# A large-kernel convolution behind an attention block: the normalization's shift put into the tap strips with a product on GpSimd and one addition on VectorE, and a last store in three transfers

## The chip, the cores and the metric

The kernel runs on one core of a Trainium2 chip. The metric is the device time of one execution in microseconds; the time before is the median of three runs.

In the names of the profile PE is TensorE (matmuls), PEld its weight loads, DVE VectorE, ACT ScalarE, POOL GpSimd, SP SyncE (here a queue that issues transfers). A name with a q behind it (SPq, POOLq) is an engine's sequencer, which issues transfers and waits for semaphores.

## What is computed

The input is one image of 384 channels and 192 x 192 pixels. The first layer adds an attention block over the channels to its normalized input (not touched here). The second normalizes its input in 32 groups, sends it through seven depthwise convolutions, each with its own batch normalization, and adds their sum to the input:

```python
x = x + _L0_conv_ref(_gn(x), ...)
x = x + _L1_conv_ref(_gn(x), ...)

def _L1_conv_ref(x, w0, ..., bn6):          # BRANCHES: (5,1) (7,1) (5,2) (3,3) (3,4) (3,5)
    out = bn_apply(dwconv(x, w0, 1), bn0)   # w0: 13 x 13
    for (k, r), w, bn in zip(BRANCHES, ws, bns):
        out = out + bn_apply(dwconv(x, w, r), bn)
    return out
```

Everything is float32. The seven convolutions fit into 13 x 13 taps, so the kernel merges them, with the batch normalizations, into one set of taps for each channel.

## The kernel before

The first 1960 us hold the statistics and the attention block; from there to 2108 us the projection (line 1459) runs, and the convolution of the second layer from 2108 us to the end. It is worked off in `NK` = 48 chunks of `CC` = 8 channels. In a chunk, a partition stands for one of `UQ` = 4 row phases, a channel and one of `NE` = 4 row ranges.

For a chunk k, these steps follow each other, spread over several iterations of the loop:

- `load_rows(k)` (lines 1288 and 1295): eight transfers on SP's queue bring the rows of the input (`raw`) and of the projection (`up`). `raw` has three buffers, `up` two. For the last chunk, one row is first cleared by a memset on POOL (line 1274).
- `load_taps(k)` (line 1310): one transfer on SP's queue brings the chunk's strips `wt` of 256 columns for each channel, three buffers. For chunk 1 it is two transfers of half the channels.
- `residual(k)` (line 1328): `raw` plus `up`, on POOL; each value of `up` is read twice in a row with a zero step. For chunks 0 and 1 it runs on DVE in pieces of 3 rows (576 elements) and a last one of 1 (192).
- `normalize1(k, i)` (line 1336), i = 0, 1, 2: scale and bias on ACT, the long part and two edge rows, into `xn` (two buffers).
- `arrange(k)` (line 1351): two DVE stream transposes from `xn` into the patches `xp` (two buffers).
- `patch(k)` (line 1318): the identity of the residual has to go through the convolution too. For this, the strips get, in the middle row block (`PAD * BC` on, 64 columns), the fixed pattern `mask` times a number for each channel, `sdb[:, cc]`, which depends on the normalization. It is eight DVE instructions of 64 columns, `w = mask * sdb + w`. The numbers `sdb` and the biases `cb` are made by `derive`, for each third of the channels, while the loops run.
- `convolve(k, c, co)` (line 1371): for each of the 8 strips c (a strip is a channel's taps), 8 matmuls; the result goes from PSUM (`l_ps`, four buffers) by an ACT eviction (line 1379) with the bias `cb` into `co` (two buffers).
- `finish(k, co, lo)` (lines 1412 and 1421): one DVE stream transpose of `co` into `o` (two buffers), and four stores on POOL's queue, one for each row phase, 32 partitions of 288 KB.

The order on every engine is the order in the program (`manual_schedule`). Iteration k of the loop on line 1530 issues `load_rows(k + 3)`, `load_taps(k + 2)` and `residual(k + 2)`, and then for c = 0 to 7 `convolve(k, c)`. At c = 0 stand, on DVE, `arrange(k + 1)`, `patch(k + 1)` and the transpose of `finish(k - 1)`, whose stores follow on POOL. The three parts of `normalize1(k + 2)` stand behind the evictions of c = 3, 4, 5 (in iteration 0: 5, 6, 7). In iteration 0, `patch(1)` is done in two halves, at c = 6 and 7. `patch(0)` lies in the projection's loop, at step `NBB + 20`.

The last chunk is convolved in two halves of the rows (`convolve_part`, line 1390, evictions on line 1403). The first half, three row blocks, is transposed and stored beside the second half's matmuls; the second half's three row blocks are transposed as two and one behind the last eviction, each with four stores over the queues of SP, ACT, POOL and SP.

Of the kernel before, what the change touches and what calls it, by code (L numbers as in the profile page):

```python
# [7 lines left out]
F32 = mybir.dt.float32  # L8
AF = mybir.ActivationFunctionType
ALU = mybir.AluOpType  # L10
# [4 lines left out]
P = 128  # L15
# [3 lines left out]
HW = H * W  # L19
# [9 lines left out]
PAD = K0 // 2  # L29
# [4 lines left out]
UQ = 4  # L34
MR = H // UQ
BR, BC = 8, 16
NT, NBQ = H // BR, W // BC
NQ = MR + 3
CC = 8
NE = 4  # L40
ME = MR // NE
TE = NT // NE
WP = W + 16
ZS = (K0 + UQ - 1) * BC
MH = UQ * BC
# [13 lines left out]
def tile_attn_then_large_kernel_conv(ctx: ExitStack, tc: tile.TileContext, a: dict, out: bass.AP):  # L59
    nc = tc.nc  # L60
    x = a["x"]
# [170 lines left out]
    o = 3 * ZQ * K0 * BC + (UQ - 1) * BC  # L232
# [58 lines left out]
    with (  # L291
# [6 lines left out]
            out=bn.rearrange("p j q i -> p j (q i)"), in_=a["bn"].rearrange("(j p) s -> p j s", p=P)  # L298
# [13 lines left out]
        for i, (k, _) in enumerate(((K0, 1),) + BRANCHES):  # L312
            wb = s1.tile([P, NJ, k, k], F32, name=f"wb{i}")
            nc.gpsimd.dma_start(
                out=wb.rearrange("p j a b -> p j (a b)"), in_=a[f"w{i}"].rearrange("(j p) s -> p j s", p=P)
# [7 lines left out]
        def load_blocks():  # L323
# [31 lines left out]
            out=wd[:, :nqk], in_=a["w_dw"][: nqk * P].rearrange("(m p) t -> p m t", p=P)  # L355
# [148 lines left out]
        for n in range(NJ * NX):  # L504
# [43 lines left out]
            if j < 2 and b == NX - 16:  # L548
                w = P * (j + 1)
# [43 lines left out]
    with ctx_v:  # L593
# [716 lines left out]
                eng.dma_start(out=wt[:, c : c + n], in_=zds[j][c0 : c0 + n].rearrange("c p z -> p c z"))  # L1310
                yield

        def patch(k, lo=0, hi=CC):

            for c in range(lo, hi):
                cc = k * CC + c
                w = taps[k][:, c, PAD * BC : (PAD + UQ) * BC]
                nc.vector.scalar_tensor_tensor(
                    w, mask.rearrange("p u x -> p (u x)"), sdb[:, cc : cc + 1], w, ALU.mult, ALU.add
                )  # L1320

        def residual(k, eng=nc.gpsimd, n=ME + 1):

# [81 lines left out]
        def finish(k, co, lo, parts=((0, TE),), engines=(nc.gpsimd,), o=None):  # L1405


            if o is None:
                o = lo.tile([P, TE, 2, W], F32, tag="o", name=f"o_{k}")
            for t0, n in parts:  # L1410
                at, of = o[:, t0], co[:, :, t0, :]
                nc.vector.transpose(  # L1412
                    bass.AP(at.tensor, at.offset, [list(at.ap[0]), [2 * W, n], [BC, NBQ], [W, 2], [1, BC]]),
                    bass.AP(
                        of.tensor,
                        of.offset,
                        [list(of.ap[0]), [NBQ, n], [1, NBQ], [NT * NBQ, CC], [TE * NBQ, NE]],
                    ),
                )
                for u in range(UQ):  # L1420
                    engines[u % len(engines)].dma_start(  # L1421
                        out=bass.AP(
                            out.tensor,
                            out.offset + k * CC * HW + (2 * u + t0 * BR) * W,
                            [[ME * UQ * W, CC * NE], [BR * W, n], [1, 2 * W]],
                        ),
                        in_=o[u * 32 : (u + 1) * 32, t0 : t0 + n].rearrange("p t y w -> p t (y w)"),
                    )
            return o
# [14 lines left out]
        with (  # L1444
            tc.tile_pool(name="by", bufs=3) as by,
            tc.tile_pool(name="b2_ps", bufs=3, space=PSUM) as b2_ps,
        ):
            stats1 = l1.tile([P, NJ, NBB, 6], F32, name="stats_t")

            for n in range(NJ * NBB):  # L1450
                i, b = divmod(n, NBB)
                if n + 4 < NJ * NBB:
                    load_sum(n + 4)
                if b == 0 and i > 0:
                    running.append(derive(i - 1, stats1))
                advance()
                ps = b2_ps.tile([P, NBK], F32, tag="pj", name="pj")
                for j in range(NJ):
                    nc.tensor.matmul(  # L1459
                        ps,  # L1460
                        lhsT=wp[:, j, i * P : (i + 1) * P],
                        rhs=v[:, j, b * RB : (b + 1) * RB, :].rearrange("p r w -> p (r w)"),
                        start=(j == 0),
                        stop=(j == NJ - 1),
                    )
                pj = by.tile([P, 2, RB // 2, WS], F32, tag="pjs", name="pjs", bufs=6)
                nc.scalar.activation(
                    pj.rearrange("p y r w -> p r y w"),
                    ps.rearrange("p (r y w) -> p r y w", y=2, w=WS),
                    AF.Identity,  # L1470
                    bias=bpj[:, i : i + 1],
                )
                t = by.tile([P, NBK], F32, tag="cell", name="cell", bufs=1)
                sm = smj.pop(n)
                nc.vector.scalar_tensor_tensor(t, sm, quarter[:, i : i + 1], ps, ALU.mult, ALU.add)
                nc.vector.bn_stats(stats1[:, i, b, :], t)
                if i == 0:
                    nc.vector.bn_stats(stats_s[:, i, b, :], sm)
                pd = pds[i]
                nc.scalar.dma_start(  # L1480
                    out=bass.AP(
                        pd.tensor,
                        pd.offset + b * NBK // 2,
                        [[HS // 2 * WS, P], [P * HS // 2 * WS, 2], [1, NBK // 2]],
                    ),
                    in_=pj.rearrange("p y r w -> p y (r w)"),
                )
                if n == NBB + 8:
                    running.append(load_rows(0, nc.gpsimd))
                if n == NBB:  # L1490
                    running.append(load_taps(0, nc.gpsimd, 1))
                if n == NBB + 14:
                    running.append(residual(0, nc.vector, 3))
                if n == NBB + 20:
                    assert not running
                    patch(0)
                    for q in range(3):
                        normalize1(0, q)
                    first = arrange(0, 1)
                if n > NBB + 20 and n % 3 < 2:  # L1500
                    next(first, None)

                if n == NBB + 22:
                    running.append(load_rows(1, nc.gpsimd))
                if n == 2 * NBB + 8:
                    second = residual(1, nc.vector, 3)
                if n >= 2 * NBB + 8 and (n % 3 == 2 or n > 2 * NBB + 16):
                    next(second, None)
                if n == 3 * NBB - 4:
                    assert next(first, first) is first and next(second, second) is second  # L1510
                if n >= 3 * NBB - 4 and n < 3 * NBB - 1:
                    normalize1(1, n - (3 * NBB - 4))
            while running:
                advance()
            running.append(derive(NJ - 1, stats1))
            advance()
# [3 lines left out]
    with (  # L1520
        tc.tile_pool(name="l2", bufs=1) as l2,
        tc.tile_pool(name="more", bufs=1) as more,
        tc.tile_pool(name="lo", bufs=2) as lo,
    ):
        pools["more"] = more
        patches(l2, 1)
        all_of(load_rows(2))
        all_of(load_taps(1, n=CC // 2))
        last = None
        for k in range(NK):  # L1530
            if k + 3 < NK:
                all_of(load_rows(k + 3))
            if k + 2 < NK:
                all_of(load_taps(k + 2))
                all_of(residual(k + 2))
            co = lo.tile([P, CC, NT, NBQ], F32, tag="co", name=f"co_{k}")
            for c in range(CC):
                if k < NK - 1:
                    convolve(k, c, co)
                else:  # L1540
                    convolve_part(k, c, co, 0, TE // 2)
                if c == CC - 2:
                    advance()
                if c == 0:
                    if k + 1 < NK:
                        all_of(arrange(k + 1))
                        if k > 0:
                            patch(k + 1)
                    if last is not None:
                        finish(k - 1, last, lo)  # L1550

                if k == 0 and c >= CC - 2:
                    patch(1, (c - CC + 2) * CC // 2, (c - CC + 3) * CC // 2)
                n = c - (CC - 3 if k == 0 else 3)
                if 0 <= n < 3 and k + 2 < NK:
                    normalize1(k + 2, n)
            last = co
        engines = (nc.sync, nc.scalar, nc.gpsimd, nc.sync)
        o = None
        for c in range(CC):  # L1560
            convolve_part(NK - 1, c, last, TE // 2, TE // 2)
            if c == 0:
                o = finish(NK - 1, last, lo, ((0, TE // 2),))
        finish(NK - 1, last, lo, ((TE // 2, 2), (TE // 2 + 2, 1)), engines, o)
        ctx_p.close()
    ctx_l1.close()

# [48 lines left out]
```

## Time and profile before

| | us |
|---|---|
| time, median of 3 runs | 2867.17 (2865.95 to 2869.23) |
| the profiled execution: time | 2862.88 |
| its span, first to last instruction | 2861.1 |
| of it from the first convolution matmul (2108.23) on | 752.9 |

Busy time of the engines in three stretches of the span (us from its start), with the mean share of the 16 DMA engines (transfers that overlap on one engine count twice):

| stretch | PE | DVE | ACT | POOL | DMA share | GB/s |
|---|---|---|---|---|---|---|
| 2030 to 2100 | 68.47 | 61.29 | 22.36 | 4.63 | 0.77 | 219 |
| 2500 to 2600 | 100.00 | 97.58 | 43.06 | 50.25 | 1.07 | 271 |
| 2800 to 2861 | 53.33 | 45.67 | 21.48 | 17.05 | 0.58 | 155 |

The groups of instructions that the change touches or stands beside, by line and form:

| line, engine, instruction | form | count | busy us | mean ns |
|---|---|---|---|---|
| L1318 DVE SCALAR_TENSOR_TENSOR, `wt` | 128x64 | 384 | 79.6 | 286 |
| L1351 DVE STREAM_TRANSPOSE, `xp` | 128x4608, whole chunk | 47 | 394.5 | 8394 |
| L1412 DVE STREAM_TRANSPOSE, `o` | 128x2304 | 47 | 206.4 | 4391 |
| L1328 POOL TENSOR_TENSOR, `raw` | 128x2496 | 46 | 230.0 | 5001 |
| L1328 DVE TENSOR_TENSOR, `raw` | 128x576 | 8 | 5.9 | 743 |
| L1328 DVE TENSOR_TENSOR, `raw` | 128x192 | 2 | 0.7 | 346 |
| L280 POOL TENSOR_TENSOR, `sum` | 128x192 | 128 | 87.9 | 687 |
| L281 POOL TENSOR_TENSOR, `sum` | 128x192 | 128 | 100.9 | 789 |
| L1421 POOL issue of a store, `out` | | 194 | 107.4 | 582 |

How to read it: the lines that follow in the next part are rows of the same profile. A row of a timeline has the start and the length in us, the engine, the line of the kernel, the instruction, what it writes from what it reads, the shape, how often (merged), and in brackets how long the engine was idle before and what ended that. A row of the waits has who waited for whom, the total in us, how often, and the longest.

### The profile page before, as it was taken

To read this page: it belongs to the slowest core of one execution; us is meant where nothing else is said; L and a number is where in the kernel's file an instruction comes from. 1 tells how busy PE (TensorE), PEld (TensorE's weight loads), DVE (VectorE), ACT (ScalarE), POOL (GpSimd) and SP (SyncE) were. 2 spreads that over 40 slices of the span, in tenths; PEclk is the share of its full clock that TensorE was granted. 3 is DMA by queue.
4 is the path that set the end of the run, shared out by engine and by line. 5 is a ranking of instruction groups with operands and counts; after the bars stand their busy time and mean duration, and the time that the engine had idled before them with its cause. 6 is when DMAs were issued, how large, how long until landed. Compare 5 with 4: busy or idle time off the path is not lost.

```text
span 2861.1 us, 37738 instructions
## 1 busy us (share of the span) xinstructions
PE 2735.6 (96%) x13662; PEld 1677.2 (59%) x13662; DVE 2498.5 (87%) x3484; ACT 1332.9 (47%) x2427; POOL 917.3 (32%) x1129
## 2 busy tenths in 40 slices
PE   0699999999999999999999999999999999999998
PEld 0356666666666666666655555545566666666666
DVE  6879998888878888788899998888789999999997
ACT  3755554444444444454444444444334444444443
POOL 4251231332323223241222222232114445444443
PEclk9899999999999999999999999999999999999999
DMA  9942432232422324232333333328889999999996
GB/s 389 419 151 65 134 114 87 81 126 72 135 74 92 111 70 137 67 126 81 100 108 107 108 109 116 115 69 234 234 206 282 270 275 275 256 271 271 270 275 168
DMA packets 269561, 475.75 MB, mean 166 GB/s; under 512 B 25858, under 2 KB 189968, under 8 KB 269248
## 3 DMA queue, kind: packets, MB, share of 16 engines
q1 hardware_dynamic: 204208, 301.51, 38.2%
q0 software_dynamic: 43328, 149.04, 15.5%
q10 hardware_dynamic: 21840, 22.81, 2.3%
q8 instruction: 108, 1.77, 0.3%
q14 instruction: 77, 0.63, 0.1%
HBM read 337.06 MB, written 136.20 MB: 165 GB/s over the span
## 4 chain that ended last, share of the span: by engine, by line
PE 85%; DVE 7%; DMA 5%; ACT 1%; issue 1%; POOL 0%; ACTq 0%; SPq 0%; DVEq 0%; POOLq 0%
PE qkv L671 51%; PE conv L1371 24%; PE pj L1459 4%; DVE v L719 3%; DMA xs<-in_x 3%; PE gram L760 2%; PE tr L748 2%; PE av L1131 1%; DVE mx L683 1%; PE qkv L429 1%; DVE acc L719 1%; DVE stats L535 1%; DMA v<-in_x 0%; DMA smj<-sums 0%; DMA wt<-zd 0%
## 5 line engine op out<-in xcount | busy, mean ns | idle before, releaser
L671 PE MATMUL qkv<-xt,wqk 128*128 128x384 f32 x3304 | 1082.5, 486 | 1.9 <-DVE mx L683 1.1
L671 PEld LDWEIGHTS qkv<-xt,wqk 128*128 128x128 f32 x3304 | 620.1, 190 | 417.1 <-DVE mx L683 4.5
L719 DVE SCALAR_TENSOR_TENSOR acc<-pooled,wd,acc 128x384 f32<-128x384 f32 (+2 forms) x1152 | 733.7, 637 | 30.6
L1371 PE MATMUL conv<-xp,wt 128*64 128x288 f32 (+1 forms) x6016 | 723.9, 404 | 2.4 <-issue 1.7
L690 ACT ACTIVATE pooled<-mx,bq 128x192 f32<-128x192 f32 x432 | 196.8, 456 | 900.2 <-DVE mx L683 898.1
L1371 PEld LDWEIGHTS conv<-xp,wt 128*64 128x64 f32 x6016 | 462.9, 137 | 260.8 <-issue 2.7
L683 DVE TENSOR_REDUCE mx<-qkv 128x192 f32<-128x768 f32 x432 | 412.3, 954 | 200.1 <-PE qkv L671 187.1
L671 PE MATMUL qkv<-xt,wv 128*128 128x384 f32 x1728 | 562.4, 487 | 2.5 <-DVE mx L683 2.2
L671 PEld LDWEIGHTS qkv<-xt,wv 128*128 128x128 f32 x1728 | 326.0, 190 | 233.4 <-DVE mx L683 9.8
L1351 DVE STREAM_TRANSPOSE xp<-xn 128x4608 f32<-128x4608 f32 (+1 forms) x107 | 445.4, 4163 | 18.0 <-PE conv L1371 10.6
L280 POOL TENSOR_TENSOR sum<-xt 128x192 f32<-128x192 f32 x128 | 87.9, 687 | 969.0 <-ACT xt L651 968.0
L719 DVE SCALAR_TENSOR_TENSOR v<-pooled,wd,v 128x384 f32<-128x384 f32 (+2 forms) x576 | 375.4, 652 | 15.2
L1379 ACT ACTIVATE co<-conv,cb 128x288 f32<-128x288 f32 x376 | 186.9, 497 | 386.1 <-PE conv L1371 381.3
L651 ACT ACTIVATE xt<-xt,gn 128x768 f32<-128x768 f32 x278 | 275.5, 1014 | 0.0
L1328 POOL TENSOR_TENSOR raw<-raw,up 128x2496 f32<-128x2496 f32 x46 | 230.0, 5001 | 38.2 <-DMA up<-pd 27.6
L1421 POOL DMA_DIRECT2D out<-o x194 | 107.4, 582 | 373.5 <-DVE o L1412 315.2
L1412 DVE STREAM_TRANSPOSE o<-co 128x2304 f32<-128x2304 f32 (+3 forms) x50 | 211.0, 4222 | 9.6 <-ACT co L1403 8.8
L1459 PE MATMUL pj<-v,wp 128*128 128x384 f32 x432 | 142.6, 489 | 1.0 <-ACT v L1138 0.7
L788 POOL DMA_DIRECT2D zd<-v x96 | 72.0, 756 | 216.1 <-ACT v L779 216.1
L1336 ACT ACTIVATE xn<-raw,par 128x2112 f32<-128x2112 f32 x48 | 103.1, 2148 | 25.4 <-POOL raw L1328 21.8
L1459 PEld LDWEIGHTS pj<-v,wp 128*128 128x128 f32 x432 | 80.9, 190 | 55.9 <-ACT v L1138 1.4
L281 POOL TENSOR_TENSOR sum<-sum,xt 128x192 f32<-128x192 f32 x128 | 100.9, 789 | 10.8
(296 smaller groups left out, 1914.6 us busy)
## 6 DMA issues: line engine op xcount, KB each, us to landing
xt<-in_x SPq DMA_DIRECT2D x96, 1152.0 KB, 7.4
raw<-in_x SPq DMA_DIRECT2D x182, 312.0 KB, 13.2
out<-o POOLq DMA_DIRECT2D x188, 288.0 KB, 8.4
wt<-zd SPq DMA_DIRECT2D x46, 1024.0 KB, 12.2
zd<-v POOLq DMA_DIRECT2D x96, 416.0 KB, 4.4
up<-pd SPq DMA_DIRECT2D x184, 156.0 KB, 12.6
xs<-in_x POOLq DMA_DIRECT2D x20, 768.0 KB, 10.7
smj<-sums SPq DMA_DIRECT2D x72, 192.0 KB, 3.0
```

The lines of the kernel that those rows point to most:

```text
L651: nc.scalar.activation(xt[:, j], xt[:, j], AF.Identity, bias=gn0[:, j, 1:2], scale=gn0[:, j, 0:1])
L671: nc.tensor.matmul(ps[:, r, : 2 * W], lhsT=wq[:, j, mm * P : (mm + 1) * P], rhs=xt[:, j, r * 2 * W : (r + 1) * 2 * W], start=(j == 0), sto ...
L683: nc.vector.tensor_reduce(mx, ps[:, :, : 2 * W].rearrange("p r (y w x) -> p r w y x", y=2, x=2), AX.XY, ALU.max,)
L690: nc.scalar.activation(pool_t[m][:, k : k + SR, 1 : 1 + WS], mx, AF.Identity, bias=bq[:, m : m + 1])
L719: nc.vector.scalar_tensor_tensor(acc[:, :nt], pool_t[m][:, k0 + dy : k0 + dy + nt, dx : dx + WS], wd[:, m, t : t + 1], acc[:, :nt], ALU.mu ...
L1328: eng.tensor_add(rv, rv, uv.unsqueeze(2).to_broadcast([P, (m1 - m0) * WS, 2]))
L1351: nc.vector.transpose(bass.AP(at.tensor, at.offset, [list(at.ap[0]), [NBQ, n], [1, NBQ], [NQ * NBQ, CC], [ME * NBQ, NE]],), bass.AP(row.te ...
L1371: nc.tensor.matmul(ps[h * MH : (h + 1) * MH, t0:t1], lhsT=wt[:, c, o : o + MH], rhs=d[:, c, g + 2 * t0 : g + 2 * t1 - 1 : 2, :], start=(e ...
L1379: nc.scalar.activation(co[:, c], ps, AF.Identity, bias=cb[:, cc : cc + 1])
L1412: nc.vector.transpose(bass.AP(at.tensor, at.offset, [list(at.ap[0]), [2 * W, n], [BC, NBQ], [W, 2], [1, BC]]), bass.AP(of.tensor, of.offse ...
L1421: engines[u % len(engines)].dma_start(out=bass.AP(out.tensor, out.offset + k * CC * HW + (2 * u + t0 * BR) * W, [[ME * UQ * W, CC * NE], [ ...
L1459: nc.tensor.matmul(ps, lhsT=wp[:, j, i * P : (i + 1) * P], rhs=v[:, j, b * RB : (b + 1) * RB, :].rearrange("p r w -> p (r w)"), start=(j = ...
```

## The change

The eight instructions of a patch become one product and one addition. `shade(k)` forms `mask` times the eight numbers of chunk k into a new tile `part` (128 x 8 x 64, one buffer) on POOL; `patch(k)` adds `part` to the strips in one DVE instruction. `shade(0)` stands ahead of `patch(0)`, and `shade(k + 1)` at the head of iteration k. `patch(1)` is no longer done in halves. `normalize1` moves from behind c = 3, 4, 5 to behind c = 4, 5, 6, except in iteration 0. For a single row block `finish` now issues one store of all 128 partitions in place of four of 32, and the last three row blocks are transposed and stored one by one; their queues are SP, SP and ACT, by `engines[t0 % len(engines)]` with t0 = 3, 4, 5.

```diff
-        def patch(k, lo=0, hi=CC):
-
-            for c in range(lo, hi):
-                cc = k * CC + c
-                w = taps[k][:, c, PAD * BC : (PAD + UQ) * BC]
-                nc.vector.scalar_tensor_tensor(
-                    w, mask.rearrange("p u x -> p (u x)"), sdb[:, cc : cc + 1], w, ALU.mult, ALU.add
-                )
+        parts = {}
+
+        def shade(k):
+
+            part = parts[k] = l1a.tile([P, CC, MH], F32, tag="part", name=f"part_{k}")
+            flat = mask.rearrange("p u x -> p (u x)")
+            nc.gpsimd.tensor_mul(
+                part,
+                flat.unsqueeze(1).to_broadcast([P, CC, MH]),
+                sdb[:, k * CC : (k + 1) * CC].unsqueeze(2).to_broadcast([P, CC, MH]),
+            )
+
+        def patch(k):
+
+            w = taps[k][:, :, PAD * BC : PAD * BC + MH]
+            nc.vector.tensor_add(w, w, parts.pop(k))
...
+                if n == 1:
+                    engines[t0 % len(engines)].dma_start(
+                        out=bass.AP(
+                            out.tensor,
+                            out.offset + k * CC * HW + t0 * BR * W,
+                            [[2 * W, UQ], [ME * UQ * W, CC * NE], [1, 2 * W]],
+                        ),
+                        in_=o[:, t0].rearrange("p y w -> p (y w)"),
+                    )
+                    continue
...
                 if n == NBB + 20:
                     assert not running
+                    shade(0)
                     patch(0)
...
         for k in range(NK):
+            if k + 1 < NK:
+                shade(k + 1)
             if k + 3 < NK:
                 all_of(load_rows(k + 3))
...
-                if k == 0 and c >= CC - 2:
-                    patch(1, (c - CC + 2) * CC // 2, (c - CC + 3) * CC // 2)
-                n = c - (CC - 3 if k == 0 else 3)
+                if k == 0 and c == CC - 1:
+                    patch(1)
+                n = c - (CC - 3 if k == 0 else 4)
...
-        finish(NK - 1, last, lo, ((TE // 2, 2), (TE // 2 + 2, 1)), engines, o)
+        finish(NK - 1, last, lo, [(t0, 1) for t0 in range(TE // 2, TE)], engines, o)
```

## Prediction

> **What bounds the kernel now.** The change touches the convolution, from 2108 us to the end, so I read the profile for that stretch: first which waits TensorE (PE) had there, then one chunk on each engine, then the start and the end of the stretch. All the waits of PE from 2108 us on are two:
>
> ```profile
> PE conv L1371 <- issue: 1.7, 1, 1.7
> PE conv L1371 <- ACT co L1379: 0.8, 1, 0.8
> ```
>
> PE loses 2.4 us in 745 us. From 2390.07 to 2837.48 us it runs 3728 matmuls with nothing between, 0.120 us each, so 15.36 us for a chunk's 128. One chunk in the timelines of VectorE (DVE) and GpSimd (POOL):
>
> ```profile
> 2771.65 4.37 DVE L1412 STREAM_TRANSPOSE o<-co 128x2304 f32<-128x2304 f32 x1
> 2776.31 9.36 DVE L1351 STREAM_TRANSPOSE xp<-xn 128x384 f32<-128x384 f32 x2 [0.29 <-PE conv L1371]
> 2785.50 1.59 DVE L1318 SCALAR_TENSOR_TENSOR wt<-mask,sdb,wt 128x64 f32<-128x64 f32 x8
> 2786.99 4.41 DVE L1412 STREAM_TRANSPOSE o<-co 128x2304 f32<-128x2304 f32 x1
> ...
> 2776.32 2.22 POOL L1421 DMA_DIRECT2D out<-o  x4 [7.64 <-DVE o L1412]
> 2778.94 4.96 POOL L1328 TENSOR_TENSOR raw<-raw,up 128x2496 f32<-128x2496 f32 x1 [0.40 <-ACT co L1379]
> ```
>
> To be seen: DVE works 9.36 + 1.59 + 4.41 us, less small overlaps, in a chunk of 15.36 us, and its only idle time, 0.29 us, ends when PE has finished reading the old patches. So PE sets the pace and DVE follows 0.3 us behind. The strips are ready at 2787.0, and PE needs them when chunk 44 begins, about 2791.4: 4.4 us of slack.
>
> The two waits of PE lie in the first chunks:
>
> ```profile
> 2120.35 4.92 POOL L1328 TENSOR_TENSOR raw<-raw,up 128x2496 f32<-128x2496 f32 x1 [11.48 <-DMA up<-pd]
> 2122.31 4.43 DVE L1318 SCALAR_TENSOR_TENSOR wt<-mask,sdb,wt 128x64 f32<-128x64 f32 x8 [0.50 <-DMA wt<-zd]
> 2125.47 15.58 PE L1371 MATMUL conv<-xp,wt 128*64 128x288 f32 x128 [1.66 <-issue]
> 2139.21 2.15 ACT L1336 ACTIVATE xn<-raw,par 128x2112 f32<-128x2112 f32 x1 [5.31 <-POOL raw L1328]
> 2141.80 2.38 PE L1371 MATMUL conv<-xp,wt 128*64 128x288 f32 x18 [0.76 <-ACT co L1379]
> ```
>
> The first strip of chunk 1 began at 2122.31 and lasted 3.06 us (the longest of line 1318; the median is 0.28). It ended 0.09 us after POOL's addition, which ran from 2120.35 to 2125.27, and PE began 0.1 us later. The same happens at 2138.73, where eight strips take 1.91 us beside a POOL addition that ends at 2139.18. The second wait: ScalarE (ACT) stood 5.31 us at a normalization that is queued ahead of the eviction PE needed.
>
> The end:
>
> ```profile
> 2853.79 2.30 DVE L1412 STREAM_TRANSPOSE o<-co 128x768 f32<-128x768 f32 x2 [5.53 <-ACT co L1403]
> 2855.37 1.76 SPq L1421 DMA_DIRECT2D out<-o  x4
> ```
>
> Two transposes, then eight stores on three queues; SP issues the last at 2856.72 to 2857.13, waits 2.4 us for stores to land (2859.5), and the span ends 1.6 us after that.
>
> **The change on DVE.** Removed: 48 groups of eight strips, 79.6 us by the costliest groups, about 1.6 us a chunk. Added: 48 additions of 128x512. The nearest rows are DVE additions of line 1328: 0.743 us for 576 elements, 0.346 for 192, so 1.034 ns an element, and 0.346 + 320 x 1.034 ns = 0.68 us for 512. DVE gains about 0.9 us a chunk, 43 us in all. On the path this is worth nothing in the steady chunks, as DVE waits for PE there: its idle 0.29 us becomes 1.2. Only if that cover were gone (PE faster than 14.5 us a chunk) would it show. Bounds for one addition: 0.66 us (512 at the 576 row's 1.29 ns an element) to 0.92 (at the 192 row's 1.80); both below 1.59. The first patch stands in the projection, at 2052.46; what it gives back there goes into DVE's next wait, 1.30 us for ACT until 2055.40.
>
> **The change on POOL.** Added: 48 products of 128x512, with both inputs spread by zero steps, which no row shows. The rows around it are the 2496-element addition (5.00 us, 2.00 ns an element, one input spread twofold) and the sums of line 281 (0.789 us for 192, 4.11 ns). Flat, these give 1.02 and 2.10 us. I take the line through 0.687 us at 192 (line 280) and 5.00 at 2496, which gives 0.69 + 320 x 1.87 ns = 1.29 us. POOL is 40 to 50% busy in the stretch, so the place matters, not the sum. The product for chunk k+1 stands at the head of iteration k, behind the four stores of the iteration before and ahead of the residual addition (L1328) for k+2. The stores wait for DVE's output transpose, which now ends 0.9 us sooner; so the stores end 0.9 sooner, the product takes 1.29, and the addition starts 0.4 us later than now or when its rows land, whichever is last. It ends some 8.3 us into the chunk; the patch comes at 9.5, the normalization later. The wait for the single buffer `part` is short: its patch was read half a chunk before. Behind the product on POOL are also the stores, the residual and, once, the memset ahead of the last chunk's rows, for which SP's queue waits (2793.82 now); 0.4 us there is covered by those rows' consumer at 2809.28.
>
> The row for a conflict is the 3.06 us strip: a DVE operation stood until a POOL operation ended. [...]
>
> **The normalization moved** one strip later (c = 4, 5, 6). Its long part can start 10.1 us into the chunk instead of 8.2, the edges end by about 14.4 (evictions come 1.92 us apart), and the next DVE transposes need them at 15.6: nothing on the path. Its rows' buffer comes free 1.92 us later; it is refilled more than ten microseconds after that (chunk 43's buffer was normalized by 2758, reloaded from 2772.26), so SP's queue doesn't feel it.
>
> **The start.** Products 0 and 1 run on an idle POOL, before 2052 and 2111. `patch(1)`, two halves before, is one addition now and waits for both halves of the taps. The second landed at 2125.47, when SP's next load was let go; the POOL addition is over at 2125.27. So the patch ends at 2125.5 + 0.7 = 2126.2, and PE starts chunk 1 0.8 us later than now. In exchange, the eviction of c = 4 no longer stands behind the normalization, and the second wait, 0.76 us, goes. Sum: 0. Bounds: -2.4 us (both waits gone) to +1.5 (the first grows by 0.8 to 1.5, the second stays).
>
> **The end.** Three transposes of 384 columns for 768 + 384: 3 x 0.82 less two overlaps of 0.08, 2.3 us again. The stores are three of 192 KB, on SP, SP and ACT, each sent as its transpose ends, at about 2854.7, 2855.4 and 2856.2, for the first at 2855.37. ACT's stores of 192 KB in the projection landed in 3.1 us (median), 2.8 us for SP's 192 KB loads there: the last lands near 2859.0 for 2859.5. I take -0.5 us; bounds 0 (the same 589 KB need the same 2.7 us of transfer, 2856.15 to 2858.85, from the last issue) and -1.1 (all of them move from 2855.4 on). [...]
>
> **Sum.** 0 in the steady chunks, 0 at the start, -0.5 at the end: the profiled execution, 2862.88 us (span 2861.1 and 1.8 around it), becomes 2862.4. The median of the runs is 4.3 us above that execution, and I keep that distance: 2866.7 us.
>
> **Rivals.** (1) DVE, not PE, sets the pace. For it: the sum of DVE's work is within 0.3 us of the chunk. Against: the 2.4 us of PE's waits. It would give 47 x 0.9 = 42 us: 2825. Chance 0.07, with anything else that saves over 5.7 us. (2) POOL and DVE in a ring become the pace: output transpose 4.40, a gap of 0.30, stores 2.22, the product, 0.1, residual 4.97, 0.1, patch 0.68, make 12.77 us plus the product. It decides from 2.6 us for the product on; at 1.29 the ring takes 14.1, at 2.10 14.9. Should the two spread inputs make it 3.5 us, each of 46 chunks takes 0.9 us more: 41 us, 2908. For it: no row shows such inputs; against: the row with one spread input is the cheapest per element. Chance 0.13, with lesser losses above 5.7 us. (3) The start loses 1.5 us and the end gains nothing: 2868.7; chance 0.08, indistinguishable from no change. (4) The product is not ahead at all, as its patch waits for it each chunk; it has until 9.5 us and ends at about 3, so this is rival 2 in its beginnings and costs nothing below the same point.
>
> **How the numbers follow.** 0.2% of the time, 5.7 us, is about what a measurement of this kernel can tell from no change. The forecast has 0.72. The bounds at start and end sum to -3.5 and +1.5 us, 2863.7 to 2868.7; the runs reach from 1.2 us below their median to 2.1 above, so the range is 2862.5 to 2870.8. It leaves out rivals 1 and 2, 0.20 together. Faster 0.07; same 0.72 + 0.08 = 0.80; slower 0.13.
>
> **What would show it.** Right: matmuls in the steady chunks still back to back at 15.36 us, DVE's wait for PE at about 1.2 us a chunk, the POOL product at 1.0 to 2.1 us, the residual addition ending before the patch, PE's first wait near 2.5 us and no second one, the last store landing 0.5 us sooner after the last matmul. Wrong: PE waiting for the patch or for evictions in the steady chunks, a patch of over 1 us (stopped by POOL), or a product above 2.6 us.

## The result and the profile after

| | before | after |
|---|---|---|
| time, median of 21 runs each | 2865.69 (2862.84 to 2869.23) | 2870.80 (2866.60 to 2875.91) |
| after to before | | 1.0018 [1.0012, 1.0024] |
| the profiled execution: span | 2861.1 | 2869.8 |
| its first convolution matmul | 2108.23 | 2110.91 |
| from there to the last half's first matmul | 729.25 | 731.39 |
| from there to the end of the span | 23.62 | 27.50 |

The change costs 5.1 us; the interval of the ratio makes that 3.4 to 6.9 us. The spans differ by 8.7 us: 2.68 before the convolution begins, 2.14 in its chunks, 3.88 at the end. I don't put the first of these down to the change: the first convolution matmul lies between 2107.0 and 2112.6 us over the profiled executions of before, after and the twelve kernels below, with no order by edit. So I read the stretches from that matmul on, and use whole times only with their intervals.

Waits of TensorE from the convolution on; columns: engine, tile and line waiting, releaser, sum in us, times, longest:

```profile
PE conv L1379 <- issue: 3.1, 1, 3.1
```

There were two of 1.7 and 0.8; now there is one, of 3.1. The steady chunks, in TensorE's timeline:

```profile
2394.89 447.58 PE L1379 MATMUL conv<-xp,wt 128*64 128x288 f32 x3728
2842.30 0.91 PE L1398 MATMUL conv<-xp,wt 128*64 128x144 f32 x12
```

The same 3728 matmuls took 447.41 us before (2390.07 to 2837.48) and take 447.41 now (2394.89 to 2842.30). One chunk in the timelines of VectorE and GpSimd:

```profile
2774.97 0.71 DVE L1328 TENSOR_TENSOR wt<-wt,part 128x512 f32<-128x512 f32 x1
2775.56 4.42 DVE L1420 STREAM_TRANSPOSE o<-co 128x2304 f32<-128x2304 f32 x1
2780.27 2.24 POOL L1439 DMA_DIRECT2D out<-o  x4 [7.16 <-DVE o L1420]
2781.13 9.36 DVE L1359 STREAM_TRANSPOSE xp<-xn 128x384 f32<-128x384 f32 x2 [1.16 <-PE conv L1379]
2782.43 1.15 POOL L1319 TENSOR_TENSOR part<-mask,sdb 128x512 f32<-128x512 f32 x1
2783.43 5.07 POOL L1336 TENSOR_TENSOR raw<-raw,up 128x2496 f32<-128x2496 f32 x1
```

The eight instructions of 1.59 us have become one of 0.71, and all that this frees stands in the bracket of the third VectorE operation: it idles 1.16 us until TensorE has read the old patches, where it was 0.29. The residual addition ends at 2788.50; the next patch comes some 1.8 us later, so the two don't meet.

The start of the convolution, from the same timelines:

```profile
2123.10 4.93 POOL L1336 TENSOR_TENSOR raw<-raw,up 128x2496 f32<-128x2496 f32 x1 [10.54 <-DMA up<-pd]
2128.78 0.69 DVE L1328 TENSOR_TENSOR wt<-wt,part 128x512 f32<-128x512 f32 x1 [4.25 <-DMA wt<-zd]
2129.57 30.71 PE L1379 MATMUL conv<-xp,wt 128*64 128x288 f32 x240 [3.08 <-issue]
```

The one addition of chunk 1 waits for the second half of the taps (4.25 us idle), starts when they are there, and TensorE follows 0.1 us behind it. But its next 240 matmuls take 30.71 us. The same 240 take 29.02 us in e12 below, where the clock stayed whole, so 1.69 us are lost here. The same stretch cut into windows (columns: busy time and count of TensorE, granted clock with 1.00 for full speed, DMA share, GB/s):

```profile
2128.00:2130.00 2.00, 0.42 (x4) 1.00 1.09 213
2130.00:2132.00 2.00, 2.00 (x13) 0.54 1.11 218
2132.00:2134.00 2.00, 2.00 (x14) 0.61 1.08 203
2134.00:2136.00 2.00, 2.00 (x20) 1.00 1.09 277
```

For 3.4 us from 2130.1 on the granted clock is half, and 13 or 14 matmuls go where 20 went. Before, behind a gap of 1.66 us, it stayed at 1.00.

The end, in the timelines of VectorE and the queues, and in windows (busy time and count of PE, PEld, DVE, ACT, POOL; then granted clock, DMA share, GB/s):

```profile
2858.61 2.36 DVE L1420 STREAM_TRANSPOSE o<-co 128x384 f32<-128x384 f32 x3 [5.53 <-ACT co L1411]
2859.50 1.32 SPq L1429 DMA_DIRECT2D out<-o  x2
2861.00 1.15 ACTq L1429 DMA_DIRECT2D out<-o  x1
```

```profile
2862.00:2864.00 2.00, 0.00 (x0) 0.00 (x0) 0.00 (x0) 0.00 (x0) 0.00 (x0) 0.50 0.26 89
2866.00:2868.00 2.00, 0.00 (x0) 0.00 (x0) 0.00 (x0) 0.00 (x0) 0.00 (x0) 0.50 0.24 90
```

The transposes and the issues are where they were expected, the last issue 2.4 us behind the first transpose. But the transfers then move some 90 GB/s with the DMA share standing at 0.26, a quarter of the 16 engines, until 2868. Before, the like stretch had a share of 0.65 to 0.81, at 167 to 218 GB/s, and was over in 3 us. One of its windows:

```profile
2857.00:2858.00 1.00, 0.00 (x0) 0.00 (x0) 0.00 (x0) 0.00 (x0) 0.00 (x0) 0.50 0.81 218
```

### The profile page after: what moved, and what is told of

It is laid out like the page before. It is cut to its first block, busy times and chain, and to the rows that moved or that the text cites. A ratio compares the mean times of both kernels' runs of the same rounds, so it can differ in the third digit from the quotient of the medians.

```text
span 2869.8 us, 37175 instructions
## 1 busy us (share of the span) xinstructions
PE 2739.0 (95%) x13662; PEld 1680.4 (59%) x13662; DVE 2452.9 (85%) x3149; ACT 1334.1 (46%) x2427; POOL 966.4 (34%) x1175
## 4 chain that ended last, share of the span: by engine, by line
PE 85%; DVE 8%; DMA 5%; ACT 1%; issue 1%; ACTq 0%; DVEq 0%; POOL 0%; SPq 0%
PE qkv L671 51%; PE conv L1379 25%; DVE v L719 3%; PE pj L1477 3%; DMA xs<-in_x 3%; PE gram L760 2%; PE tr L748 2%; DVE mx L683 1%; PE av L1131 1%; PE qkv L429 1%; DVE acc L719 1%; DMA smj<-sums 1%; DVE stats L535 1%; PE conv L1398 1%; DMA sm<-sums 0%
## 5 line engine op out<-in xcount | busy, mean ns | idle before, releaser
L1420 DVE STREAM_TRANSPOSE o<-co 128x2304 f32<-128x2304 f32 (+2 forms) x51 | 211.1, 4143 | 10.5 <-ACT co L1411 8.8
```

What stands on the lines that cost most here:

```text
L1420: nc.vector.transpose(bass.AP(at.tensor, at.offset, [list(at.ap[0]), [2 * W, n], [BC, NBQ], [W, 2], [1, BC]]), bass.AP(of.tensor, of.offse ...
```

## The experiments

In the expectations "theory" and "rival" are those of each run. The table puts all of them side by side: the two stretches of the profiled execution, TensorE's first wait in the chunks, the median, and the ratio to the kernel before, which ran beside them on the same chip (its medians there: 2865.81 for e1 to e4, 2866.25 for e5 to e8, 2866.40 for e9 to e12). The ratio and its 95% interval are those of the measurement, not the quotient of the medians; where the two part, as for e5 and e10, neither says much alone.

| kernel | to the last half | from there to the end | first wait | median (runs) | ratio to before |
|---|---|---|---|---|---|
| before | 729.25 | 23.62 | 1.66 | | |
| after | 731.39 | 27.50 | 3.08 | 2870.80 (21) | 1.0018 [1.0012, 1.0024] |
| e1 | 735.87 | 23.68 | 3.78 | 2866.57 (11) | 1.0001 [0.9990, 1.0011] |
| e2 | 730.26 | 27.50 | 1.60 | 2869.26 (12) | 1.0012 [0.9996, 1.0028] |
| e3 | 728.84 | 27.51 | 2.03 | 2868.00 (11) | 1.0013 [1.0001, 1.0025] |
| e4 | 731.27 | 21.83 | 2.96 | 2864.35 (11) | 0.9994 [0.9986, 1.0003] |
| e5 | 731.05 | 23.06 | 3.11 | 2866.61 (11) | 1.0010 [0.9998, 1.0021] |
| e6 | 732.72 | 23.71 | 0 | 2863.96 (11) | 0.9993 [0.9984, 1.0002] |
| e7 | 728.26 | 23.56 | 1.52 | 2866.20 (1) | |
| e8 | 742.11 | 27.28 | 2.92 | 2878.32 (4) | 1.0049 [1.0035, 1.0063] |
| e9 | 730.72 | 27.15 | 2.42 | 2869.86 (12) | 1.0010 [0.9999, 1.0020] |
| e10 | 729.96 | 23.20 | 1.81 | 2864.34 (12) | 0.9984 [0.9967, 1.0000] |
| e11 | 728.17 | 23.09 | 0.28 | 2863.78 (12) | 0.9982 [0.9965, 1.0000] |
| e12 | 728.29 | 23.21 | 1.67 | 2864.29 (12) | 0.9994 [0.9981, 1.0006] |

### e1 and e2: which half of the change loses

e1 is the changed kernel with the end of before; e2 is before with the new end alone.

```diff
 e1, against after
-                if n == 1:
-                    engines[t0 % len(engines)].dma_start(
...
-                    continue
-        finish(NK - 1, last, lo, [(t0, 1) for t0 in range(TE // 2, TE)], engines, o)
+        finish(NK - 1, last, lo, ((TE // 2, 2), (TE // 2 + 2, 1)), engines, o)
 e2, against before: the same lines the other way round, all else as before
```

> The changed kernel with the end of the kernel before: transposes of 2 and 1 row blocks and eight stores of 32 partitions. Theory (tail): the three stores of 128 partitions move their 589 KB at some 95 GB/s and cost 3.9 us at the end (27.5 us from the last half's first matmul to the end of the span against 23.6), so this kernel is 3.9 us below the changed one, about 1 to 2 us above the kernel before, and the stretch from the first matmul of line 1398 to the end is 23.6 us again. Rival (start): the loss is PE's longer first wait and the half clock behind it, and the tail is noise of one execution: then this kernel stays 4 to 5 us above the kernel before.

> The kernel before with the three last stores of 128 partitions and nothing else of the change. Tail theory: 3.9 us above the kernel before (ratio 1.0014), 27.5 us from the last half's first matmul to the end. Start theory: within 1 us of the kernel before, 23 to 24 us at the end.

e2 carries the long end on its own: 27.50 us, as after, and SyncE's last waits are the same. The waits of SyncE's queue for stores to land, at the end of e2:

```profile
SPq L1622 <- DMA out<-o: 7.6, 3, 3.4
```

These are the 7.6 us in three waits that after has too (before: 2.4 in one). e2's median stands 3.5 us above before's, but its interval, 0.9996 to 1.0028, takes in no loss: it is the profile, more than the time, that shows the long end. e1 has the short end back, 23.68 us. Its median stands 0.8 us above before's, and its interval, 0.9990 to 1.0011, takes in no loss as well as 3 us. Its profiled execution is slower than after's in the chunks: first wait 3.78 us with the half clock behind it, and three more waits of TensorE, 2.9 us together, for strips that VectorE could add to only when late taps had landed. The medians don't show such a loss, so it is scatter in the main; but the chunks are not as safe from late taps as the profile of before made them look. Waits of TensorE for strips in the chunks stand in the profiles of three kernels with single products (e1, e6, e10) and in none of the four without products (before, e2, e7, e12). One execution of each doesn't settle whether the products have a part in them, and no run tested it.

### e3: the first addition in two halves

```diff
-        def patch(k):
-            w = taps[k][:, :, PAD * BC : PAD * BC + MH]
-            nc.vector.tensor_add(w, w, parts.pop(k))
+        def patch(k, lo=0, hi=CC):
+            w = taps[k][:, lo:hi, PAD * BC : PAD * BC + MH]
+            nc.vector.tensor_add(w, w, parts[k][:, lo:hi])
...
-                if k == 0 and c == CC - 1:
-                    patch(1)
+                if k == 0 and c >= CC - 2:
+                    patch(1, (c - CC + 2) * CC // 2, (c - CC + 3) * CC // 2)
```

> The changed kernel with patch(1) as two additions of four strips each, as the kernel before had it. If the patch's wait for the second half of the taps makes PE's first wait long, the first addition now ends 0.3 to 0.5 us after GpSimd's residual addition, PE's wait falls from 3.1 to about 2.0 us, the clock stays at 1.00 behind it, and the time falls by 1.1 us of wait and 1.5 us of clock, 2.6 us together. If the wait is a matter of the residual addition alone (the two exclude each other), both additions wait equally and PE's wait stays near 3 us; the time stays within 1 us of the changed kernel's.

The timelines of VectorE and TensorE:

```profile
2125.02 2.34 DVE L1328 TENSOR_TENSOR wt<-wt,part 128x256 f32<-128x256 f32 x1 [1.56 <-DMA wt<-zd]
2128.04 0.42 DVE L1328 TENSOR_TENSOR wt<-wt,part 128x256 f32<-128x256 f32 x1 [0.68 <-DMA wt<-zd]
2127.46 29.21 PE L1379 MATMUL conv<-xp,wt 128*64 128x288 f32 x240 [2.03 <-issue]
```

The first four strips no longer wait for the second half of the taps. The gap falls by 1.05 us, and the 240 matmuls behind it take 29.21 us for 30.71: together the 2.55 us by which this stretch is shorter than after's (728.84 for 731.39). The first half takes 2.34 us where the second takes 0.42. In e10 below, which has the same halves, the first takes 3.08 us and ends at 2128.13, 0.29 us after GpSimd's residual addition (2122.91 to 2127.84), for which it stands, as the strips of before did. In the time the edit can't be told from after: 1.0013 [1.0001, 1.0025] beside 1.0018.

### e4 and e5: what makes the end long

e4 sends the three last stores into flat scratch buffers in DRAM, 128 rows of 1536 bytes each; it leaves the last three row blocks of the last chunk out of the output. e5 keeps the three transposes, each followed by four stores of 32 partitions.

```diff
 e4
                 if n == 1:
                     engines[t0 % len(engines)].dma_start(
-                        out=bass.AP(
-                            out.tensor,
-                            out.offset + k * CC * HW + t0 * BR * W,
-                            [[2 * W, UQ], [ME * UQ * W, CC * NE], [1, 2 * W]],
-                        ),
+                        out=flat[t0 % 3],
                         in_=o[:, t0].rearrange("p y w -> p (y w)"),
                     )
                     continue
 e5: this branch is left out
```

> The changed kernel whose three last stores go to three scratch tensors of 128 rows of 384 values in DRAM, so that the destination's slowest dimension is 128 and not 4; the same 192 KB each, the same queues. It leaves the last three row blocks of the last chunk out of the output. If the slow stores come from that dimension of 4 (the DMA share stood at 0.26, four engines of sixteen), the share rises to about 0.8 or more, the last store lands within 3.5 us of its issue, and the end takes 22.5 to 23.5 us from the first matmul of the last half instead of 27.5. If 128 partitions or three large transfers are slow as such, it stays at 27 us or more. [...]

> The changed kernel with its three single transposes at the end, but four stores of 32 partitions behind each, twelve in all, over SP, ACT, POOL and SP. The destination's slowest dimension is 32. If the dimension of 4 alone made the end slow, the end takes 23 to 23.8 us from the last half's first matmul (kernel before 23.62, three stores over sixteen engines 21.83), and the time is some 4 us below the changed kernel's. If it is the one-by-one transposes or the earlier stores that are slow, it stays at 27.

With the same queues, sizes, issues and source, and another shape of the destination, the end of e4 is 5.67 us shorter than after's; that is below the 22.5 to 23.5 us expected. Its windows, columns as above:

```profile
2857.00:2858.00 1.00, 0.00 (x0) 0.00 (x0) 0.84 (x2) 0.00 (x0) 0.00 (x0) 0.68 0.58 207
2858.00:2859.00 1.00, 0.00 (x0) 0.00 (x0) 0.00 (x0) 0.00 (x0) 0.00 (x0) 0.50 0.78 284
2859.00:2860.00 1.00, 0.00 (x0) 0.00 (x0) 0.00 (x0) 0.00 (x0) 0.00 (x0) 0.50 0.28 98
```

The share goes to 0.78 and the rate to 284 GB/s, three times after's. The destination of after's stores is written `[[2 * W, UQ], [ME * UQ * W, CC * NE], [1, 2 * W]]`: its slowest dimension is the 4 row phases. e4's has 128 there, and the stores of before and of e5 have 32. Four of 16 engines would be a share of 0.25; after's stood at 0.26. The packets of the last stores, in after and in e4, differ as well:

```profile
DMA packets 396, 0.59 MB, mean 50 GB/s; under 512 B 12, under 2 KB 396, under 8 KB 396
DMA packets 432, 0.59 MB, mean 118 GB/s; under 512 B 48, under 2 KB 432, under 8 KB 432
```

Both move 384 rows of 1536 bytes. The packets under 512 bytes beside them are 12 for after's three stores, 4 each, and 48 for e4's, 16 each. The eight stores of before have 128 and the twelve of e10 have 192, again 16 each; in after and before these packets have 4 bytes. So in these four runs the count goes with the slowest dimension (4 for one of 4, 16 for one of 32 or 128), and not with the 128 partitions or with the number of stores.

The shares go the same way: 0.24 to 0.27 at 89 to 98 GB/s where the slowest dimension is 4 (after and, from 2860 to 2864 us, e2), 0.65 to 0.81 where it is 32 (before) and 0.78 where it is 128 (e4). Destinations with another slowest dimension were not run.

e4 also has its rows one behind the other in DRAM, which after has not. e5 answers that: it writes the same scattered rows as after, with destinations of 32, and its end takes 23.06 us, 0.56 us less than before's, with single transposes and four more issues.

The times go the same way. With three stores of after's shape (after, e2, e3, e9) the medians lie 2.2 to 5.1 us above before's; with any other end (e1, e4, e5, e6, e7, e10, e11, e12) they lie between 2.6 us below and 0.8 us above. e8, with its threefold products, is left out.

### e9: the same stores from GpSimd

```diff
-        finish(NK - 1, last, lo, [(t0, 1) for t0 in range(TE // 2, TE)], engines, o)
+        finish(NK - 1, last, lo, [(t0, 1) for t0 in range(TE // 2, TE)], o=o)
```

> The changed kernel with its three last stores all issued by GpSimd, same addresses and shapes. Theory (a store whose DRAM side has 4 as its slowest dimension is spread over 4 of the 16 DMA engines, whoever issues it): the DMA share in the tail stays near 0.26 and the time from the last half's first matmul to the end of the span stays at 27 us or more. Rival (the spreading belongs to the queues of SyncE and ScalarE, and GpSimd's descriptors are spread otherwise): the share rises above 0.6 and that stretch falls to 22 to 23.7 us. [...]

Neither of the two held. e9's windows:

```profile
2861.00:2863.00 2.00, 0.00 (x0) 0.00 (x0) 0.00 (x0) 0.00 (x0) 0.00 (x0) 0.50 0.53 123
2863.00:2865.00 2.00, 0.00 (x0) 0.00 (x0) 0.00 (x0) 0.00 (x0) 0.00 (x0) 0.50 0.36 124
```

The share rises to 0.53 (0.62 in one half microsecond), twice the 0.26 of after's stores of the same shape on the queues of SyncE and ScalarE. But the end is 27.15 us all the same, at 124 GB/s. Of the 576 packets 444 were under 512 bytes, where after had 12 of 396; nearly all of the 0.59 MB went in the other 132, some 4.5 KB each in the mean, where after had 384 of 1.5 KB. So the shape costs as much from this queue, in another way; what the small packets are, and whether they are the cost, was not followed up.

### e7 and e12: without the products

e7 is before with the normalization one strip later and nothing else; e12 is e7 with twelve stores of 32 partitions.

```diff
 e7 and e12, against before
-                n = c - (CC - 3 if k == 0 else 3)
+                n = c - (CC - 3 if k == 0 else 4)
 e12 also
-        finish(NK - 1, last, lo, ((TE // 2, 2), (TE // 2 + 2, 1)), engines, o)
+        finish(NK - 1, last, lo, [(t0, 1) for t0 in range(TE // 2, TE)], engines, o)
```

> The kernel before with the normalization behind c = 4, 5, 6 and nothing else. Theory: PE's second wait (0.76 us, and 1.81 in the kernel with the new stores alone) is the eviction queued behind the normalization; here it is gone, the first wait stays at 1.6 to 1.7 us and the steady chunks at 15.36 us. Rival: the wait comes from the taps or the transposes, and stays.

> The kernel before, with only the normalization one strip later and twelve stores of 32 partitions at the end: no products on GpSimd, the strips as before on VectorE. Theory (the products and the single addition are worth nothing, since VectorE waits for PE in the steady chunks): within 1 us of the kernel with halves and twelve stores; 728.3 us to the last half and 23.1 us from there. Rival (VectorE's relief is worth something): 2 us or more slower than that kernel.

TensorE's waits in e7 from the convolution on:

```profile
PE conv L1371 <- issue: 1.5, 1, 1.5
```

The second wait, 0.8 us for an eviction, is gone, so it is the move of the normalization that takes it away; the stretch is 0.99 us shorter than before's. The break cost more than the 0.76 us that its row shows as a wait: before's 128 matmuls ahead of it take 16.33 us up to the next one (2125.47 to 2141.80), 0.97 us more than the 15.36 of an unbroken chunk. e12, without products, has the median 2864.29; e10, with them, has 2864.34 on the same chip, and the 3728 steady matmuls take 447.41 us in both. The relief of VectorE by 0.9 us a chunk brings nothing that can be seen here.

### e8: the product three times

```diff
+            for _ in range(1 if k < 2 else 3):
                 nc.gpsimd.tensor_mul(
                     part,
...
```

> The changed kernel with each product on GpSimd done three times (from chunk 2 on), so that the product's place takes 3.4 us instead of 1.14; the values are the same. The ring of the prediction (output transpose 4.40, gap 0.30, stores 2.22, product, 0.1, residual 4.97, 0.1, patch 0.68) makes 12.77 + 3.4 = 16.2 us, 0.8 us over the chunk: some 37 us over 46 chunks, about 2907 us, with PE waiting for patches. If a patch is not stopped by a residual addition on GpSimd, nothing of this closes the ring and the time stays within 2 us of the changed kernel's.

The timelines of VectorE and GpSimd, over one chunk:

```profile
2500.74 4.41 DVE L1421 STREAM_TRANSPOSE o<-co 128x2304 f32<-128x2304 f32 x1
2505.44 2.24 POOL L1440 DMA_DIRECT2D out<-o  x4 [5.18 <-DVE o L1421]
2507.60 3.39 POOL L1320 TENSOR_TENSOR part<-mask,sdb 128x512 f32<-128x512 f32 x3
2510.95 4.95 POOL L1337 TENSOR_TENSOR raw<-raw,up 128x2496 f32<-128x2496 f32 x1
2514.21 2.24 DVE L1329 TENSOR_TENSOR wt<-wt,part 128x512 f32<-128x512 f32 x1
2516.37 4.42 DVE L1421 STREAM_TRANSPOSE o<-co 128x2304 f32<-128x2304 f32 x1
```

This is the ring of the second rival, closed. The addition takes 2.24 us for 0.68: it begins at 2514.21 and ends 0.5 us after GpSimd's, and the output transpose, which lets the next stores go, is late. From one transpose to the next are 15.63 us for 15.36. The expectation had 16.2 us and 2907 us in all; 0.27 us a chunk is a third of the price it named, and the median is 2878.32, 12 us above before's. Less the products' 3.39 the 15.63 leave 12.24 us for the rest of the ring, so 3.1 us for the product is, by this estimate, the point from which it decides; the one of the change takes 1.14.

### e6, e10 and e11: repairs of the start and the end

e10 is e3's halves with e5's twelve stores. e11 also cuts the residual addition of chunk 2 on GpSimd into pieces of 7 and 6 rows. e6 has the halves and the pieces, with before's end.

```diff
 e6 and e11
-                all_of(residual(k + 2))
+                all_of(residual(k + 2, n=7 if k == 0 else ME + 1))
```

> The changed kernel with the old end, patch(1) in two additions, and the residual addition of chunk 2 on GpSimd in two pieces (7 and 6 rows). If a patch and a residual addition exclude each other for a whole instruction, the first addition of patch(1) can now go in between the pieces: it ends at most 3 us after the first half of the taps has landed and PE's first wait falls from 2.0 us (two halves, residual in one piece) to 0.5 to 1.5 us. If the taps alone hold PE, the wait stays at 2.0 us. The time is 1 to 2 us below the kernel before, if nothing else moves.

> The changed kernel with the first chunks' addition in two halves, and twelve stores of 32 partitions at the end. Theory (the loss is the start and the end alone, and the products are worth nothing): first wait of PE about 2.0 us with the clock at 1.00 behind it, 728.8 us from the convolution's first matmul to the last half, 23.1 us from there to the end, together 1 us less than before's 729.25 + 23.62; runs 0 to 2 us below before's median. Rival (the products cost time in the steady chunks that the start hid): 730 us or more and no better than before.

> The kernel with halves and twelve stores, and the residual addition on GpSimd for chunk 2 in two pieces of 7 and 6 row blocks, so that the first half's addition of strips can run between them. Theory (the first wait is an addition on VectorE held until GpSimd's addition ends): the first addition takes about 1.4 us and starts near 2121, PE's first wait goes from 2.0 to 1 us or less, and the time falls by up to 1 us against the kernel without the split. Rival (the taps' transfers are what is late next): the first wait goes, and PE waits as much for strips in the chunks after it; no difference within 1 us.

e10's end is as short as expected, 23.20 us, but it takes 729.96 us to the last half, not 728.8: two waits in later chunks, 0.50 us for strips and 0.26 us for an eviction, came on top. That is the 730 us that its rival asked for, in one execution; the median, equal to e12's, doesn't go with the rival.

The first half's addition in e10, and then the start in e11, from the timelines of GpSimd, VectorE and TensorE:

```profile
2125.05 3.08 DVE L1328 TENSOR_TENSOR wt<-wt,part 128x256 f32<-128x256 f32 x1 [0.61 <-DMA wt<-zd]
```

```profile
2120.87 5.26 POOL L1336 TENSOR_TENSOR raw<-raw,up 128x1344 f32<-128x1344 f32 x2 [11.08 <-DMA up<-pd]
2123.04 0.86 DVE L1328 TENSOR_TENSOR wt<-wt,part 128x256 f32<-128x256 f32 x1 [1.32 <-DMA wt<-zd]
2124.00 4.06 PE L1379 MATMUL conv<-xp,wt 128*64 128x288 f32 x32 [0.28 <-issue]
```

With a seam in GpSimd's addition the first half of the strips is done at 2123.9, and the first wait of TensorE is 0.28 us where e10 has 1.81. That VectorE's addition stands here until GpSimd's instruction has ended is thereby shown: with the one in two pieces, the other takes 0.86 us where it took 3.08 in e10. Little of it reaches the time: the medians of e10 and e11 are 0.56 us apart. Behind the start TensorE waits 0.69 us for an eviction, and VectorE waits for the taps of later chunks more often. It waited for taps 27 times in e11 (36.6 us) and 9 times in e10 (13.6 us), while the DMA engines moved 265 to 269 GB/s between 2170 and 2830 us in before, after, e1 to e7 and e10 to e12. e6 repeats this: no first wait, then 4.1 us of TensorE's waits in five places, and 34 waits of VectorE for taps (44.3 us). That the transfers, and not the strips, bound any further gain at the start is my reading of this; no run tested it.

e10 and e11 are 2 to 2.6 us below before in the medians; their intervals end at 1.0000, and e12 is as good without products. None is shown to be faster than before.

## Why the prediction failed, step by step

**The end** is the step that failed: "I take -0.5 us; bounds 0 (the same 589 KB need the same 2.7 us of transfer, 2856.15 to 2858.85, from the last issue) and -1.1". It measured +3.88, outside both bounds, and e2 and e4 show why (an end of 27.50 us in e2 as in after; 12 small packets in after for 48 in e4, a share of 0.26 for 0.78). The upper bound took it for granted that the new stores move bytes at the rate of the old ones, and the duration, 3.1 us for 192 KB, came from the projection's stores, whose destination has the 128 partitions as its slowest dimension. The three stores had a destination whose slowest dimension is 4, and ran with the DMA share at 0.26. The sum has the transposes (2.36 us for 2.3) and the issues right; only the rate is wrong, some 95 GB/s for 218.

What decided is how the destination is written, and the diff shows that: `[2 * W, UQ]` stands first. With 128 there, the 128-partition stores of e4 end 1.23 us sooner (21.83 us) than the 32-partition ones of e5 (23.06); whether the partitions, the number of stores or the flat destination do that was not separated.

**The start** was put at 0, from +0.8 at the first wait and -0.76 at the second. The mechanism was right: the wait is for both halves of the taps, and e3 takes 1.05 us of it back. The second wait went as forecast, and with it 0.97 us of time. The first term was mis-sized, +1.42 for +0.8, mostly since in this execution the taps landed 17.8 us after the first matmul, where the profile of before had 17.2; such moments vary between executions (first waits of 2.42 to 3.78 us in the kernels with this start). And a term was missing: the half clock behind the gap, 1.69 us. Together 1.42 - 0.97 + 1.69 make the +2.14 us of the stretch, above the bound of +1.5. Whether the half clock comes is partly luck: e8, with the same start and a gap of 2.92 us, kept the whole clock (last section).

**The steady chunks**, 0: right. 447.41 us both times; VectorE's wait for TensorE is 1.16 us in the chunk shown for the 1.2 forecast. The addition takes 0.678 us in the mean for 0.68, the product 1.136 for 1.29. e12 beside e10 shows no worth of the relief in the time either.

**The normalization**, nothing on the path: right, by e7.

**The rivals.** That VectorE sets the pace fell with the 447.41 us and with e12. The ring of GpSimd and VectorE exists, and closes from about 3.1 us on by e8, where the prediction said 2.6: it counted 0.78 us for the addition and the gap ahead of it, of which only 0.47 us lie behind the residual addition's end, and small gaps where the trace has small overlaps. The conflict of the two engines is not new with the change: the old strips stood for GpSimd as well (3.06 us), so it does not speak against the change alone. What the loss looked like, 1.0018, was in no rival: the nearest, the third, let the end gain nothing and stopped there.

**The sum** by what was measured: 0 in the chunks, +2.1 at the start, +3.9 at the end make +6.0 for this execution, beside 5.1 [3.4, 6.9] in the runs. Of the two, only the end repeats in every profile that has these stores (27.28 to 27.51 with SyncE's and ScalarE's queues). The start's share in the runs is not settled: e1, which has it alone, lies 0.8 us above before with an interval of -2.9 to +3.2 us.

## What to carry to other kernels

Before stores are merged into fewer, larger ones, look at the first dimension of the address pattern in DRAM as well as at the partitions: 4 there cost 3.9 us on 589 KB. When two half waits are merged into one on the engine that sets the pace, price the longer gap with the half-clock stretch that may follow it: here 3.41 us at half clock cost 1.3 to 1.7 us behind gaps of 2.42 to 3.78 us. And work taken from an engine that waits for another each round only lengthens its wait: here 0.29 us became 1.16 and the time of a chunk stayed.

## What was not expected of the hardware

From 1912 us on, the granted clock of TensorE fell to a half behind gaps of 2.17 to 3.78 us between matmuls, but not behind all of them: 2.17 (e2), 2.19 (e6), 2.29 (e4), 2.37 (e11), 2.46 (e1) and 2.92 us (e8) left it whole. The half clock lasted 3.41 us each time up to the last half (once, in e7, twice that), which cost 1.3 to 1.7 us at the start of the convolution (240 matmuls in 30.34 us in e5 and 30.71 in after, for 29.02 in e12).

What decides is not the length of a gap alone. All changes of the clock in a trace lie whole multiples of 3.413 us apart; after has them at 1908.28, 1911.69, 1928.76, 1932.17, 2130.14, 2133.55 and 2860.59 us, which is 1, 5, 1, 58, 1 and 213 of them; before has them at 1907.83, 1911.24 and 2856.74 us, 1 and 277. So I divided each of the 14 traces into windows by its own grid, from 1912 us to the last half, and added up the time without a matmul in those that began at the whole clock. All 14 windows with 2.10 us or more were followed by a half clock. Of the others, up to 2.06 us, two were: 1.34 and 1.36 us (e1, e10), with four matmuls of one column each beside. The gap of 3.08 us in after lies in one window but for 0.24 us. That of 2.92 us in e8 straddles two, with 1.19 and 1.73 us. Where the grid lies differs from one execution to the next: counted from the span's start, after's lies 0.44 us behind before's. What sets it was not followed up.

One half clock lies in code that the change doesn't touch: behind a gap of 2.35 us, at 1928.8 to 1932.2 us of after. Before, the gaps there were 1.81 and 2.01 us and the clock stayed at 1.00. By an estimate, half of the 3.41 us at half clock, it can account for 1.7 of the 2.68 us by which that execution's convolution began later.
